# Queries and keys of three of four head groups as seven block products instead of eight

## The chip, the cores and the metric

The kernel runs on one core of one Trainium2 chip, as one program that computes the whole block for eight batches. The metric is the device time of one execution in microseconds (us). A core has five engines that run side by side and meet through semaphores: TensorE (PE, matmuls into the eight PSUM banks), VectorE (DVE), ScalarE (ACT), GpSimd (POOL), and SyncE (SP), which here issues the DMAs. [...]

## The reference

An attention block and a feed-forward block, both with a layer norm before and after and a residual sum, in float32. Batches B=8, positions S=1024, model width D=512, 16 heads of 32, feed-forward width 2048.

```python
qvk = (layernorm(x) @ Wqvk).reshape(b, s, 3, H, HD)
q, v, k = qvk[:, :, 0], qvk[:, :, 1], qvk[:, :, 2]
scores = (einsum('bshi,bthi->bsth', q, k) + causal_mask) / sqrt(d)
weights = softmax(scores, axis=2)
x = x + layernorm(einsum('bsth,bthi->bshi', weights, v).reshape(b, s, d) @ Wo)
hidden = layernorm(x) @ W1 + b1
act = relu(hidden + coef * sin(theta + hidden * 0.1))      # coef from the parameters
x = x + layernorm(act @ W2 + b2)
```

The change is about `q` and `k`, the first line of this.

## The kernel before, in words

The sixteen heads are worked on in four groups of four (`g` = 0 to 3), so that the 128 columns of a group's queries fill the 128 partitions, head by head in rows of 32. For each batch `attention` walks through the four groups; the feed-forward of the batch follows, and within it the end of the attention of this batch and the preparation of the next are interleaved.

**Order.** PE, DVE, ACT and POOL run their instructions in the order in which the program text issues them (`in_order`). Work is written as Python generators; `advance(work, n)` issues the next `n` steps of one between other instructions. So what stands next to what is written by hand. While group g is in attention, the generator `project_qkv(b, g + 1)` (or the first group of the next batch) is drawn step by step as filler between the score units.

**One group.** `find_maxima` first computes scores query by key (matmuls at L575) in seven units of four PSUM banks each, in four runs (`MAX_RUNS`): the first run is one unit, the other three are two units each. DVE takes the row maxima out of the banks (L593 and L605), and ACT exponentials of the first half give row sums (L625). After run n, `advance(work, MAX_FILL[g > 0][n])` draws filler. Then the maxima are split into three bf16 parts (on POOL for the first half of the queries) and transposed on PE (L115). Two further units of scores (`MAX_LATE`) come a little later, `later(0)` and `later(1)`.

Then `weigh` computes the scores transposed, key by query, with the maxima folded in by a bf16 matmul (L681, then L692), in ten units (`KEY_UNITS`, counted by `at`): three for the first half of the queries, seven for the second. ACT exponentiates them out of PSUM (L707), POOL sets what lies above the diagonal to zero (`affine_select`, L711), and one unit later PE multiplies them with the values (L730, `flush`). In the second half DVE also adds up the weights (L759), which PE sums over partitions at the start of the next group (L745).

**The projection before.** Queries and keys of a group are each two halves of 512 positions. Each is four matmuls of 128x128 by 512 (the four row blocks of the 512 input features), accumulated in one bank (L477) and copied to SBUF by ACT with the scale (L488). Each takes two steps of filler, two matmuls a step. Values are four steps (L497, L505), two blocks of 128 positions each. A matmul in float32 shows as two records in the trace.

**PSUM.** `psum` hands out banks at build time, in the order of the program: the one that was released longest ago. A unit of scores takes four of the eight banks.

**Other users of the same engines.** In batch 0 `mix_weights` prepares the feed-forward weights with 32 POOL operations of 128x512 (L284) and stores them, one step per weigh unit. The feed-forward works with seven products for eight already, for both of its matrices (`w1_mixed`, `w2_mixed`), its sums made on DVE and POOL (L1125 for the activations).

Of the kernel before, what the change touches and what calls it, by code (L numbers as in the profile page):

```python
# [11 lines left out]
F32 = mybir.dt.float32  # L12
# [20 lines left out]
def kernel(  # L33
# [24 lines left out]
    NG = NH // HPG  # L58
    QSCALE = 1.0 / math.sqrt(D)

# [6 lines left out]
    tp = ctx.enter_context(tc.tile_pool(name="tp", bufs=4))  # L67
    pp = ctx.enter_context(tc.tile_pool(name="pp", bufs=19))
    tmp = ctx.enter_context(tc.tile_pool(name="tmp", bufs=5))
    small = ctx.enter_context(tc.tile_pool(name="small", bufs=4))  # L70
    wp = ctx.enter_context(tc.tile_pool(name="wp", bufs=WEIGHTS))
    mixp = ctx.enter_context(tc.tile_pool(name="mixp", bufs=2))
    sump = ctx.enter_context(tc.tile_pool(name="sump", bufs=4))
# [37 lines left out]
    def in_order(instruction):  # L111
        tc.keep_in_program_order(instruction)
# [20 lines left out]
    w1_mixed = dram.tile([NSTEP, len(PRODUCTS), P, 2 * 2 * P], F32, tag="w1m", name="w1_mixed")  # L133
    w2_mixed = dram.tile([NSTEP, len(PRODUCTS2), P, 2 * QUART], F32, tag="w2m", name="w2_mixed")
    wqvk_v = w_qvk.rearrange("(kc p) n -> p kc n", p=P)

# [5 lines left out]
    def fetch(b, g, queue=nc.sync):  # L142

        for part in (0, 1, 2):
            w_of[b, g, part] = w_tile([KC, P], "wqvk")
            c0 = part * D + g * P
            queue.dma_start(w_of[b, g, part], wqvk_v[:, :, c0 : c0 + P])

    fetch(0, 0, nc.scalar)
# [215 lines left out]
    def advance(work, steps=1):  # L365
        for _ in range(steps):
            if next(work, None) is None:
                return

    def finish(work):  # L370
        for _ in work:
            pass
# [22 lines left out]
    def norm1_first():  # L395

        dst = new_xnT(0)
        return staged(NT, *norm_stages(lambda t: xt[0, t], dst, nc.scalar.copy))

    moments_ahead = {}  # L400

# [59 lines left out]
    def project_qkv(b, g):  # L461
# [11 lines left out]
        def queries_or_keys(n, half):  # L473
            pq = psum([P, HALF])
            for kc in range(KC):
                in_order(
                    nc.tensor.matmul(  # L477
                        pq,
                        w_of[b, g, 2 * n][:, kc, :],
                        xnT[b, half][:, kc, :],  # L480
                        start=(kc == 0),
                        stop=(kc == KC - 1),
                    )
                )
                if kc == 1:
                    yield True
            dst = qk[b, g][n][:, half * HALF : (half + 1) * HALF]
            in_order(nc.scalar.activation(dst, pq, AF.Copy, scale=1.0 if n else -QSCALE))  # L488
            drained(pq)
            yield True  # L490

        def values(t0):
# [12 lines left out]
            in_order(nc.scalar.copy(v[b, g][:, t0 : t0 + 2, :], pv))  # L505
            drained(pv)
            yield True

        yield from queries_or_keys(0, 0)
        yield from values(0)  # L510
        yield from queries_or_keys(1, 0)
        yield from queries_or_keys(0, 1)
        yield from queries_or_keys(1, 1)
        for t0 in (2, 4, 6):
            yield from values(t0)

# [8 lines left out]

    MAX_FILL = ((3, 2, 2, 2), (1, 2, 2, 2))

# [239 lines left out]
    def attention(b, wvT, after):  # L770
# [24 lines left out]
        for g in range(NG):  # L795
            more, first = after(g)
            mT, later = find_maxima(b, g, work, sums, more if first is None else iter(()))
            mTs = [mT]
            at = 0
            for c in range(2):  # L800
# [3 lines left out]
                for u, keys in enumerate(units):  # L804
                    later(at)
                    weights, placed = weigh(b, g, c, keys, mTs[c])
                    if at < 2:
                        advance(work)
# [6 lines left out]
                    if c and u == len(units) - 2:  # L815
                        finish(work)
                        work = projections(g + 1)
                    if c and u >= len(units) - 2:
                        advance(work)
# [51 lines left out]
    def finish_block(b, half, wvT, x2T, mixed, out_w):  # L871


        x2T[half] = tp.tile([P, KC, HALF], F32, tag="t", name=f"x2T_{b}_{half}")
        mixed[half] = mixp.tile([P, 3, 2, QUART], F32, tag="mix", name=f"mix_{b}_{half}")
        ys, xns, mvs, rss = {}, {}, {}, {}
# [48 lines left out]
        def mix(t):  # L925
# [5 lines left out]
            b12, b22 = right[:, :2], right[:, 2:]  # L931
            m1, m2, m4 = (mixed[half][:, n, :, t * P : (t + 1) * P] for n in range(3))
            subtract = lambda *a: in_order(nc.gpsimd.tensor_tensor(*a, ALU.subtract))
# [8 lines left out]
    def feed_forward(b, x2T, mixed, before, between):  # L942
# [49 lines left out]
        def product(bank, s, name, first=False):  # L992
# [6 lines left out]
                "3": x[:, 2:, QUART:],  # L999
                "4": m[:, 2],  # L1000
                "5": m[:, 0],
                "6": m[:, 1],
                "7": x[:, :2, QUART:],
# [247 lines left out]
        advance(between)  # L1251
        finish(before)
        units = second()
        advance(units)
        for s, quota in enumerate(SECOND):
# [3 lines left out]
            for n, more in enumerate(quota):  # L1259
# [9 lines left out]
                if s == STEPS and n == 3 and b + 1 < B:  # L1269
                    fetch(b + 1, 1)  # L1270
        finish(measuring)
        while len(quarters) > 1:
            advance_ends(1)
# [4 lines left out]
    advance(first_norm, TPB + 4)  # L1278
    for _ in range(TPB):
        advance(work)  # L1280
        advance(first_norm)
    finish(first_norm)
    advance(work, 4)
    prepare_parameters()
# [71 lines left out]
```

## Time and profile before

| | |
|---|---|
| median of 3 runs | 3681.44 us (3680.97 to 3681.45) |
| the profiled execution | 3681.3 us |
| its span, first to last instruction | 3679.6 us |
| PE busy | 3601.1 us, 98% |
| DVE busy | 2680.4 us, 73% |
| ACT busy | 1408.2 us, 38% |
| POOL busy | 1133.8 us, 31% |
| mean granted clock of PE | 0.997 |

A row of a group gives the line, the engine, the operation, output and input tiles with their shapes and the number of records; then the busy time of all and the mean of one in ns; then the engine's idle time before them and what ended it. A row of the timeline gives start and duration in us, the engine, line and operation, and the number of records merged; in brackets the idle time before it and what ended that. A row of the windows gives the stretch, its length, then the busy time of PE, PE's weight loads, DVE, ACT and POOL, then the granted clock of PE (1.00 is full), the DMA share and GB/s. Ends of matmuls are modelled, and a matmul that waits for a bank can show as a long matmul.

### The profile page before, as it was taken

To read this page: it belongs to the slowest core of one execution; us is meant where nothing else is said; L and a number is where in the kernel's file an instruction comes from. 1 tells how busy PE (TensorE), PEld (TensorE's weight loads), DVE (VectorE), ACT (ScalarE), POOL (GpSimd) and SP (SyncE) were. 2 spreads that over 40 slices of the span, in tenths; PEclk is the share of its full clock that TensorE was granted. 3 is DMA by queue.
4 is the path that set the end of the run, shared out by engine and by line. 5 is a ranking of instruction groups with operands and counts; after the bars stand their busy time and mean duration, and the time that the engine had idled before them with its cause. 6 is when DMAs were issued, how large, how long until landed. Compare 5 with 4: busy or idle time off the path is not lost.

```text
span 3679.6 us, 61558 instructions
## 1 busy us (share of the span) xinstructions
PE 3601.1 (98%) x22721; PEld 2357.4 (64%) x22721; DVE 2680.4 (73%) x5571; ACT 1408.2 (38%) x2708; POOL 1133.8 (31%) x1740
## 2 busy tenths in 40 slices
PE   8999999999999999999999999999999999999998
PEld 4447864478654786548854488544885458854587
DVE  5877867678676786767867678776787767777775
ACT  4552135621355213652146521465114642156410
POOL 2333432134311343113431234222342223422243
PEclk9999999999999999999999999999999999999999
DMA  4444751047510574105841068310683116820176
GB/s 137 142 141 132 243 192 34 20 146 249 175 41 10 158 258 154 41 10 172 266 132 41 13 185 269 112 41 18 198 275 92 38 33 199 262 70 13 47 220 197
DMA packets 305084, 476.21 MB, mean 129 GB/s; under 512 B 29136, under 2 KB 90640, under 8 KB 304784
## 3 DMA queue, kind: packets, MB, share of 16 engines
q1 hardware_dynamic: 302624, 470.44, 40.8%
q8 instruction: 181, 2.97, 0.3%
q10 hardware_dynamic: 2160, 1.84, 0.2%
q14 instruction: 119, 0.97, 0.1%
HBM read 440.70 MB, written 31.46 MB: 128 GB/s over the span
## 4 chain that ended last, share of the span: by engine, by line
PE 83%; DVE 11%; ACT 2%; POOL 2%; issue 1%; DMA 0%; POOLq 0%; DVEq 0%; SPq 0%; ACTq 0%
PE banks L1144 16%; PE banks L1009 15%; PE banks L477 13%; PE banks L575 8%; PE banks L730 7%; PE banks L692 7%; PE banks L497 7%; PE banks L897 6%; PE banks L681 3%; PE banks L115 2%; DVE u L1036 2%; DVE hid L1052 2%; DVE u L1030 1%; PE banks L745 1%; DVE hid L1058 1%; ACT w L707 1%
## 5 line engine op out<-in xcount | busy, mean ns | idle before, releaser
L707 ACT ACTIVATE w<-banks 128x1024 f32<-128x1024 f32 (+1 forms) x640 | 566.6, 939 | 296.1 <-PE banks L692 296.0
L759 DVE TENSOR_TENSOR w<-w 128x1024 f32<-128x1024 f32 (+3 forms) x400 | 421.9, 1099 | 186.7 <-PE banks L730 151.8
L711 POOL TENSOR_SCALAR_AFFINE_SELECT w<-w 128x256 f32<-128x256 f32 x512 | 287.3, 578 | 847.2 <-ACT w L707 839.8
L605 DVE CUSTOM_DVE_ANT_0 es<-banks,mask 128x128 f32<-128x128 f32 (+3 forms) x1024 | 432.5, 485 | 102.6 <-PE banks L575 102.6
L1009 PE MATMUL banks<-x2T,wm 128*128 128x256 f32 x2048 | 477.3, 381 | 28.1 <-DVE u L1079 13.6
L477 PE MATMUL banks<-xnT,wqvk 128*128 128x512 f32 x1024 | 481.3, 609 | 0.7 <-ACT xnT L342 0.7
L1144 PE MATMUL banks<-wm,hm 128*128 128x256 f32 x2048 | 470.4, 380 | 2.3 <-POOL hm L1125 2.3
L1037 ACT ACTIVATE u<-u 128x1024 f32<-128x1024 f32 x128 | 135.3, 1057 | 852.1 <-DVE u L1036 803.5
L1009 PEld LDWEIGHTS banks<-x2T,wm 128*128 128x128 f32 x2048 | 386.7, 190 | 91.0 <-DVE u L1079 16.8
L1144 PEld LDWEIGHTS banks<-wm,hm 128*128 128x128 f32 x2048 | 388.0, 190 | 56.4 <-POOL hm L1125 5.5
L593 DVE TENSOR_REDUCE mx<-banks 128x1 f32<-128x512 f32 (+1 forms) x384 | 309.8, 862 | 109.1 <-PE banks L575 109.1
L1144 PE MATMUL banks<-wm,hid 128*128 128x256 f32 x1536 | 357.7, 379 | 0.0
L1009 PE MATMUL banks<-mix,wm 128*128 128x256 f32 x1536 | 354.6, 380 | 2.3 <-DVE u L1079 2.3
L1125 POOL TENSOR_TENSOR hm<-hid 128x256 f32<-128x256 f32 x256 | 204.0, 797 | 456.2 <-DVE hid L1058 437.9
L477 PEld LDWEIGHTS banks<-xnT,wqvk 128*128 128x128 f32 x1024 | 182.8, 190 | 239.1 <-issue 184.5
L692 PE MATMUL banks<-q,k 32*128 32x512 f32 (+3 forms) x3072 | 329.6, 491 | 0.0
L730 PE MATMUL banks<-w,v 128*32 128x512 f32 (+3 forms) x3072 | 318.5, 495 | 5.4 <-POOL w L711 5.4
L1009 PEld LDWEIGHTS banks<-mix,wm 128*128 128x128 f32 x1536 | 291.1, 190 | 50.6 <-issue 7.6
L575 PE MATMUL banks<-k,q 32*128 32x512 f32 (+3 forms) x3072 | 322.0, 513 | 0.4 <-DVE mx L605 0.2
L1144 PEld LDWEIGHTS banks<-wm,hid 128*128 128x128 f32 x1536 | 292.4, 190 | 39.1
L625 ACT ACTIVATE es<-es,mx 128x512 f32<-128x512 f32 (+3 forms) x512 | 279.6, 550 | 2.1 <-DVE mx L605 2.1
L497 PEld LDWEIGHTS banks<-wqvk,xnT 128*128 128x128 f32 x2048 | 239.3, 192 | 51.6 <-issue 24.4
(114 smaller groups left out, 4322.9 us busy)
## 6 DMA issues: line engine op xcount, KB each, us to landing
wm<-w_mixed SPq DMA_DIRECT2D x1344, 256.0 KB, 3.1
xin<-in_L_attn_h_dram SPq DMA_DIRECT2D x112, 256.0 KB, 3.8
wqvk<-in_L_attn_Wqvk_dram SPq DMA_DIRECT2D x93, 256.0 KB, 5.2
out_dram<-x SPq DMA_DIRECT2D x64, 256.0 KB, 2.1
x<-in_L_attn_h_dram SPq DMA_DIRECT2D x60, 256.0 KB, 3.1
w_mixed<-w_t SPq DMA_DIRECT2D x56, 256.0 KB, 3.0
wo<-in_L_attn_Wo_dram SPq DMA_DIRECT2D x32, 256.0 KB, 5.0
w_t<-in_L_ffn_W_dram SPq DMA_DIRECT2D x32, 128.0 KB, 4.0
```

The lines of the kernel that those rows point to most:

```text
L477: nc.tensor.matmul(pq, w_of[b, g, 2 * n][:, kc, :], xnT[b, half][:, kc, :], start=(kc == 0), stop=(kc == KC - 1),)
L497: nc.tensor.matmul(pv[:, t - t0, :], xnT[b, t // TPB][:, kc, (t % TPB) * P : (t % TPB + 1) * P], w_of[b, g, 1][:, kc, :], start=(kc == 0), ...
L575: nc.tensor.matmul(scs[j // 2][:, j % 2, at : at + n], queries[r, i * P : (i + 1) * P], keys[r, k0 : k0 + n], start=True, stop=True,)
L593: nc.vector.tensor_reduce(out=mx[:, m], in_=sc[:, m, cols], op=ALU.min, axis=mybir.AxisListType.X,)
L605: nc.vector.tensor_tensor_reduce(out=es[:, m, cols], in0=sc[:, m, cols], in1=mask[:, HALF - n :], scale=1.0, scalar=FMAX, op0=ALU.add, op1 ...
L692: nc.tensor.matmul(sts[j // 2][:, j % 2, cols], all_keys[r, kb * P : (kb + 1) * P], all_queries[r, q0 : q0 + n], start=False, stop=True,)
L707: in_order(nc.scalar.activation(w[:, :, :width], st[:, :, :width], AF.Exp, scale=-1.0))
L711: select = nc.gpsimd.affine_select(out=square, in_=square, compare_op=ALU.is_ge, fill=0.0, base=0, pattern=[[0, 2], [1, P]], channel_multi ...
L730: nc.tensor.matmul(acc[r, HALF - n :], v[b, g][:, kb, r], weights[j // 2][:, j % 2, cols], start=first and k == 0, stop=last and k == len( ...
L759: in_order(nc.vector.tensor_add(t[:, :, q], t[:, :, q], w[:, :, cols]))
L1009: nc.tensor.matmul(bank[:, n, :], w[:, n, kc, :], moving[:, kc, :], start=first and kc == 0 and n == 0, stop=kc == 1 and n == 1, skip_grou ...
L1144: nc.tensor.matmul(region, a[:, n], w[:, n], start=start and n == 0, stop=last and n == 1, skip_group_check=True,)
```

## The change

The eight block products of a group's queries and keys (two halves of the input features, two halves of the positions, queries and keys) become seven, by the scheme of Strassen and Winograd, for the groups 1, 2 and 3 of each batch. Group 0 is projected as before, though in whole steps.

- Four sums of blocks of the normalised input (`mix_x`, eight POOL operations of 128x512) are made once a batch: for batch 0 before the first group, for the others in the last two steps of the feed-forward of the batch before.
- Four sums of the weights of a group (`mix_weights_of_group`, four POOL operations of 128x256) are made in batch 0, stored to DRAM and fetched again for each later batch, two more loads of 256 KB a group.
- Each of the seven products is two matmuls into a bank of its own. ACT copies it to SBUF with the scale, and POOL makes the sums, seven operations of 128x512 a group. The scale 1/sqrt(D) is split evenly over queries and keys.
- The filler now has eight steps, not twelve: values, two products, values, values, two products, values, two products, one product. `MAX_FILL` and the places in `attention` where filler is drawn are changed to suit.
- The pool `pp` has 24 buffers, not 19; the feed-forward's `mixed` tiles lie in it too, and the pool `mixp` is gone.

```diff
-    QSCALE = 1.0 / math.sqrt(D)
+    HALF_SCALE = float(D) ** -0.25
-    pp = ctx.enter_context(tc.tile_pool(name="pp", bufs=19))
+    pp = ctx.enter_context(tc.tile_pool(name="pp", bufs=24))
-    mixp = ctx.enter_context(tc.tile_pool(name="mixp", bufs=2))
+    qk_mixed = dram.tile([NG, 2, P, 4 * P], F32, tag="qkm", name="qk_mixed")
...
+        if b and g:
+            for n in range(2):
+                w_of[b, g, "mix", n] = w_tile([4 * P], "wmix")
+                queue.dma_start(w_of[b, g, "mix", n], qk_mixed[g, n])
...
+    def mix_weights_of_group(b, g):
...
+        pool(s12[:, near], wk[:, near], wk[:, far], ALU.add)
+        pool(s12[:, far], s12[:, near], wq[:, near], ALU.subtract)
+        pool(s34[:, near], wq[:, near], wk[:, near], ALU.subtract)
+        pool(s34[:, far], wq[:, far], s12[:, far], ALU.subtract)
+        for n in range(2):
+            nc.sync.dma_start(qk_mixed[g, n], w_of[b, g, "mix", n])
+    def mix_x(b):
...
+        for to, left, right in ((t1, b12, b11), (t2, b22, t1), (t3, b22, b12), (t4, b21, t2)):
+            for kc in range(2):
+                in_order(
+                    nc.gpsimd.tensor_tensor(to[:, kc], left[:, kc], right[:, kc], ALU.subtract)
+                )
+                yield True
...
+        def product(w, kc0, moving, dst, sign=1.0):
+            pq = psum([P, HALF])
+            for kc in range(2):
+                in_order(nc.tensor.matmul(pq, w[:, kc0 + kc, :], moving[:, kc, :],
+                                          start=kc == 0, stop=kc == 1))
+            in_order(nc.scalar.activation(dst, pq, AF.Copy, scale=sign * HALF_SCALE))
+            drained(pq)
+        def blocks():
...
+            product(wq, 0, xnT[b, 0][:, :2, :], p1)
+            product(s12, 2, t2, p6)
+            add(p6, p6, p1)
+            u2 = p6
+            yield True
+            values(2)
+            yield True
+            values(4)
+            yield True
+            p2, p7 = pair()
+            product(wq, 2, xnT[b, 0][:, 2:, :], p2, -1.0)
+            product(s34, 0, t3, p7)
+            subtract(queries[:, near], p2, p1)
+            add(p7, p7, u2)
+            u3 = p7
+            yield True
+            values(6)
+            yield True
+            p5, p4 = pair()
+            product(s12, 0, t1, p5)
+            product(wk, 2, t4, p4)
+            add(keys[:, near], p4, u3)
+            add(keys[:, far], p5, u3)
+            add(p5, p5, u2)
+            u4 = p5
+            yield True
+            p3, _ = pair()
+            product(s34, 2, xnT[b, 1][:, 2:, :], p3, -1.0)
+            subtract(queries[:, far], p3, u4)
+            yield True
+        values(0)
+        yield True
+        if g:
+            yield from blocks()
+        else:
...
-    MAX_FILL = ((3, 2, 2, 2), (1, 2, 2, 2))
+    MAX_FILL = ((2, 1, 1, 1), (1, 1, 1, 1))
...
+            if not b and g + 2 < NG:
+                mix_weights_of_group(b, g + 2)
...
-                    if at < 2:
+                    if at in (1, 4):
                         advance(work)
...
-                    if c and u >= len(units) - 2:
+                    if c and u == len(units) - 1:
                         advance(work)
...
+        mixing_x = mix_x(b + 1) if b + 1 < B else iter(())
...
+                if s >= STEPS - 1:
+                    advance(mixing_x)
```

## The prediction

> **What bounds the kernel now.** I read the page first, then the timeline of TensorE and VectorE in one attention group, then the same stretch where the kernel happens to have no filler.
>
> ```profile
> PE 3601.1 (98%) x22721; PEld 2357.4 (64%) x22721; DVE 2680.4 (73%) x5571; ACT 1408.2 (38%) x2708; POOL 1133.8 (31%) x1740
> L477 PE MATMUL banks<-xnT,wqvk 128*128 128x512 f32 x1024 | 481.3, 609 | 0.7 <-ACT xnT L342 0.7
> ```
>
> TensorE (PE) is busy 98% of the span; the query and key products (L477) are 481.3 us of it. The profiled run took 3681.3 us, its span 3679.6; the median of the runs is 3681.44, so sums made on the span carry over as they stand. Does PE set the time in each stretch? The windows of two equal stretches (first score unit to the first late pair of units: maxima and their filler) say no:
>
> ```profile
> core 0: us, PE busy (x) PEld busy (x) DVE busy (x) ACT busy (x) POOL busy (x), PEclk, DMA share, GB/s
> 1468.82:1497.97 29.15, 29.15 (x219) 16.00 (x217) 22.77 (x77) 15.46 (x44) 2.26 (x8) 1.00 0.07 19
> 3390.19:3414.67 24.48, 23.96 (x147) 13.00 (x145) 23.81 (x79) 13.01 (x38) 2.25 (x8) 0.79 0.00 1
> ```
>
> The second is the last group of the last batch, with nothing left to project. Without the 16.7 us of projections that the first one holds, it is only 4.7 us shorter: VectorE (DVE), busy 23.81 of 24.48, is the bound there. PE still reads 98% busy, so its busy share does not show waiting. The kernel is PE-bound only because each filler is as long as DVE needs:
>
> ```profile
> 1472.87 2.00 PE L575 MATMUL banks<-k,q 32*128 32x512 f32 x16
> 1474.80 3.70 PE L477 MATMUL banks<-xnT,wqvk 128*128 128x512 f32 x8
> 1478.43 2.00 PE L575 MATMUL banks<-k,q 32*128 32x512 f32 x24
> 1474.03 2.42 DVE L593 TENSOR_REDUCE mx<-banks 128x1 f32<-128x512 f32 x3 [0.60 <-PE banks L575]
> 1479.59 2.42 DVE L593 TENSOR_REDUCE mx<-banks 128x1 f32<-128x512 f32 x3 [0.70 <-PE banks L575]
> ```
>
> Scores and filler take PE 5.56 us (1472.87 to 1478.43); DVE, 1.16 us behind, needs 4.84 for that run's maxima (1474.03 to 1478.87) and 5.17 for the next (1479.59 to 1484.76). It idles 0.4 to 0.7 a run. There is no more slack than that.
>
> **Saved.** 481.3/1024 is 0.470 us a record, two records per matmul; a product over two 128-row blocks is four records, 1.88 us. Seven for eight in 24 groups (three of four, eight batches): -45.1 us.
>
> **The maxima.** The new fills after runs 0 to 3 are two products, values, values, two products: 3.63, 1.98, 1.98, 3.53 us, where 1.98 and three times 3.6 stood. With run 0 at time 0, run 1 now starts at 1.08+0.99+3.63=5.70 (before 4.05); DVE starts at 6.86 and has freed run 2's last bank at 6.86+4.84+5.17=16.87. PE wants that bank for the second half of run 3 at 5.70+1.93+1.98+1.94+1.98+0.97=14.50. Eight banks, four to a unit, leave no other. The wait is 2.4 us, of which I give 0.3 back because the other heads' matmuls overlap it: 2.05 us x 24 = 49.2. The group that projects for the next batch keeps a key filler of 3.63 between: 0.8 x 7 = 5.6.
>
> **The late pair.**
>
> ```profile
> 1491.63 1.14 PE L575 MATMUL banks<-k,q 32*128 32x512 f32 x8
> 1492.59 0.40 PE L681 MATMUL banks<-mT,minus 32*128 32x512 bf16 x4
> 1492.81 1.04 PE L692 MATMUL banks<-q,k 32*128 32x512 f32 x8
> 1493.78 2.05 PE L497 MATMUL banks<-wqvk,xnT 128*128 128x128 f32 x16
> 1495.76 1.14 PE L575 MATMUL banks<-k,q 32*128 32x512 f32 x8
> ```
>
> The order of the changed program has no values product (L497) between the two late units, and both use the same four banks. DVE frees the fourth 1.16+2.45=3.6 us after the first unit starts; PE is back after 2.15 (1491.63 to 1493.78). Wait 1.5, less 0.5 of overlap: 1.0 us x 24 groups; 0.1 in the seven where next-batch transposes stand between. 24.7.
>
> **The sums on Pool.** Seven 128x512 operations a group. Four stand where Pool is idle. Three (both halves of the keys, then u4) are queued behind the copy of p4 and ahead of the two selects of the third unit of weights; PE's weighted values wait for those. The row for such an operation:
>
> ```profile
> L284 POOL TENSOR_TENSOR w_t<-w_t x32: 1257/1274/2277, 73.8 to 253.7; 128x512 f32<-128x512 f32 x32
> ```
>
> PE gets there 0.99+0.66+0.32+1.00+1.19=4.2 us after p4; Pool after 0.77 (copy) + 3x1.26 + 0.85 (two selects) = 5.4: 1.2 us x 17 groups, 0.25 x 7 under transposes: 22.2. I take 1.26, since DVE idles there now (5.12 us before 1507.66); at 2.28 it is 3.1 more a group, +52, kept for the upper end. [...]
>
> **The tail.** The last two units had two half products (1.91 each) as cover for exponentials and selects; now one values product. The last batch shows this place with no cover:
>
> ```profile
> 3383.76 1.81 PE L730 MATMUL banks<-w,v 128*32 128x512 f32 x8
> ...
> 3387.48 1.06 PE L730 MATMUL banks<-w,v 128*32 128x384 f32 x12 [0.48 <-POOL w L711]
> 3389.09 1.17 PE L730 MATMUL banks<-w,v 128*32 128x256 f32 x8 [0.56 <-POOL w L711]
> 3390.19 1.15 PE L575 MATMUL banks<-k,q 32*128 32x128 f32 x16
> ```
>
> 3383.76 to 3390.19 is 6.43 us, against 6.91 (1515.74 to 1522.65) with 3.82 of filler in it. Removing all of it gains 0.5, so removing 1.84 gains no more: charge 1.84-0.5=1.3 x 16, 0.2 x 7 beside transposes: 22.2. The 0.23 us wait for ScalarE after the third unit goes where PE comes later anyway: -5.5.
>
> **At nothing.** Three more copies a group (3x0.60=1.8 us) on ScalarE, 32.55 of 53.83 us busy; if it were late, 1.8x24=43. Mixing the next batch's input, eight Pool operations (10.1 us) in the last feed-forward steps: by the program's order those sums are issued dozens of matmuls (77 x 0.466=36 us in one case) ahead of use; uncovered, 7x10.1=71. Two more loads a group and six stores on SP's queue, a group (54 us) ahead against 5.2 us to land; their 42 loads would cost at most that each, 218. Four weight sums of 0.73 before the first selects of batch 0, where Pool waits 6.2. Pool in batch 0 already carries the feed-forward's weights and makes groups 1.9 to 4.4 us longer (58.18 against 53.83 in the second group): +6, between 0 and a repeat of 13.
>
> **Sum.** -45.1+54.8+24.7+22.2+22.2-5.5+6=+79, so 3760 us. Half the waits would leave +17, 3698.
>
> **Rivals.** *PE-bound throughout:* the waits fall into the pipelining of matmuls, and the saving arrives: 3681-45=3636. For it: in the second group PE's waits now sum to 0.23 of 53.83 us. Against: the unfilled stretch. It decides when the waits of a group sum to under 1.88 us; I have about 5. *The clock falls as well:* batch 0 shows a Pool wait of 1.96 us and what follows:
>
> ```profile
> 95.00:99.50 4.50, 2.54 (x36) 1.30 (x36) 4.10 (x5) 0.52 (x1) 4.50 (x5) 1.00 0.60 190
> 99.50:103.00 3.50, 3.50 (x19) 0.97 (x12) 3.50 (x16) 0.47 (x1) 0.45 (x1) 0.51 0.73 203
> ```
>
> The granted clock is 0.51 after it; scores and sums took 3.51 us (98.90 to 102.41) where 2.07 is usual (1468.82 to 1470.89). Once in each of 24 groups: +35, 3795; with Pool at 2.28 as well, 3847. My waits come in pieces of 0.3 to 1.2 us and the 1.5 us one at 156 left the clock alone, so this is not the likeliest. [...] *It does not do what it says:* the built order does have 14 matmuls for 16 in those groups, so no chance is left for this.
>
> **Chances.** Forecast 0.6, clock or contention on top 0.2, PE-bound throughout 0.12, something between with half the waits or fewer 0.08. Range 3695 (half the waits) to 3825 (clock and part of the contention). A difference of 0.2%, 7.4 us, is about what can be told from no change: faster 0.12, same 0.03, slower 0.85.
>
> **What would show it.** The group from one first score unit to the next, 53.83 us in the second group of a batch, should read about 57.3 (-1.9, +2.05, +1.0, +1.2, +1.3, -0.2). DVE should run without a gap from run 1 to run 3, PE show waits on maxima before run 3 and the second late unit, and on Pool's select at the third unit. From the fourth group's first scores to the next batch's, 285.0 us now, should be some 288.6 (1.8 of filler that the group before no longer takes, 0.8, 1.0), with nothing from the feed-forward in it. A group of 52 us would prove the rival right; a clock under 0.98 over the span, the other.

## The result, and the profile after

The changed kernel takes 3837.32 us (median of four runs, 3837.12 to 3838.48), 1.042 times the time before (95% interval 1.041 to 1.044). That is 155.9 us slower; the forecast was 79 us slower, and the time lies above its range. The profiled execution spans 3835.7 us. The page and the groups of TensorE rows (busy time of all in us, mean of one in ns, then idle time and its releaser):

```profile
PE 3703.1 (97%) x22625; PEld 2411.8 (63%) x22625; DVE 2732.2 (71%) x5571; ACT 1450.6 (38%) x2780; POOL 1467.1 (38%) x1984
...
L672 PE MATMUL banks<-k,q 32*128 32x512 f32 (+3 forms) x3072 | 430.5, 522 | 0.7 <-DVE mx L702 0.6
...
L827 PE MATMUL banks<-w,v 128*32 128x512 f32 (+3 forms) x3072 | 352.2, 498 | 41.6 <-POOL w L808 41.3
```

The rows of before that answer to the last two, the scores and the weighted values:

```profile
L575 PE MATMUL banks<-k,q 32*128 32x512 f32 (+3 forms) x3072 | 322.0, 513 | 0.4 <-DVE mx L605 0.2
...
L730 PE MATMUL banks<-w,v 128*32 128x512 f32 (+3 forms) x3072 | 318.5, 495 | 5.4 <-POOL w L711 5.4
```

PE holds 96 records fewer and is busy 102 us more. The same 3072 records of scores went from 322.0 to 430.5 us with hardly any idle time in front (0.4 and 0.7): that is the wait for banks that DVE has not yet read, and it shows as long matmuls, not as idle time (the waits are read one by one below, and the run named *late* takes one of them away). The wait of the weighted values for Pool's selects does show, 5.4 to 41.3.

Where the 156.2 us between the two spans lie, from the first score unit of each group:

| | before | after | difference |
|---|---|---|---|
| start to first scores | 39.4 | 36.8 | -2.6 |
| batch 0 | 464.2 | 495.9 | +31.7 |
| batches 1 to 6, each | 453.8 | 472.4 | +18.6 (112.5 in all) |
| of these: groups 1, 2, 3 | 57.6, 53.8, 57.4 | 61.1, 58.4, 59.4 | +3.5, +4.6, +1.9 |
| fourth group to the feed-forward | 73.7 | 79.3 | +5.6 |
| feed-forward to the next batch | 211.2 | 214.3 | +3.0 |
| batch 7 | 454.3 | 468.9 | +14.6 |

In batch 6 the difference is 19.3, as the end of its feed-forward was 1.2 us shorter before and only 0.6 now, so the six add up to 112.5. The first row is no gain of the change: the same beginning read 37.5 to 39.1 us in *late*, *adds*, *tail* and *nomixx* below. In the second group of batch 3 (first scores at 1538.71) the waits can be read one by one. Timeline, TensorE and VectorE, maxima:

```profile
1546.34 2.05 PE L530 MATMUL banks<-wqvk,xnT 128*128 128x128 f32 x16
1548.32 3.30 PE L672 MATMUL banks<-k,q 32*128 32x512 f32 x24
1551.56 2.05 PE L530 MATMUL banks<-wqvk,xnT 128*128 128x128 f32 x16
1553.54 3.18 PE L672 MATMUL banks<-k,q 32*128 32x512 f32 x24
1556.64 1.98 PE L545 MATMUL banks<-xnT,wqvk 128*128 128x512 f32 x4
...
1555.43 2.42 DVE L690 TENSOR_REDUCE mx<-banks 128x1 f32<-128x512 f32 x3
```

The same two runs before (the first starts at 1478.43, a row that the prediction shows):

```profile
1480.37 3.70 PE L477 MATMUL banks<-xnT,wqvk 128*128 128x512 f32 x8
1484.00 2.01 PE L575 MATMUL banks<-k,q 32*128 32x512 f32 x24
1485.94 3.70 PE L477 MATMUL banks<-xnT,wqvk 128*128 128x512 f32 x8
```

Runs 2 and 3, twenty-four records of scores each, took 1.94 us before and now take 3.24 and 3.10, counted to the start of the next fill: 1.30 and 1.17 of waiting, together 2.47 us. DVE's reduction at 1555.43 has no idle time in brackets, where the rows shown of before had 0.60 and 0.70: DVE is the bound here. The late pair of units, same view:

```profile
1562.34 1.14 PE L672 MATMUL banks<-k,q 32*128 32x512 f32 x8
...
1563.52 1.04 PE L789 MATMUL banks<-q,k 32*128 32x512 f32 x8
1564.38 2.40 PE L672 MATMUL banks<-k,q 32*128 32x512 f32 x7
...
1568.27 1.98 PE L545 MATMUL banks<-xm,wmix 128*128 128x512 f32 x4
```

Where the next fill stood before (the second unit starts at 1495.76, in the prediction's rows):

```profile
1497.97 2.05 PE L497 MATMUL banks<-wqvk,xnT 128*128 128x128 f32 x16
```

From the second unit of scores to the next fill 3.89 us, where 2.21 stood (1495.76 to 1497.97): 1.68 us. Pool's sums and the third unit of weights:

```profile
1572.76 2.50 POOL L565 TENSOR_TENSOR k<-blocks 128x512 f32<-128x512 f32 x2 [1.84 <-ACT blocks L553]
1575.33 1.26 POOL L565 TENSOR_TENSOR blocks<-blocks 128x512 f32<-128x512 f32 x1
1576.55 0.77 POOL L808 TENSOR_SCALAR_AFFINE_SELECT w<-w 128x256 f32<-128x256 f32 x2
...
1577.01 0.99 PE L827 MATMUL banks<-w,v 128*32 128x256 f32 x8 [0.87 <-POOL w L808]
```

Three sums run back to back in front of the two selects, and PE waits 0.87 us for these. Before, the only wait of PE near there was one of 0.23 us for ScalarE:

```profile
1505.31 0.39 PE L681 MATMUL banks<-mT,minus 32*128 32x512 bf16 x2 [0.23 <-ACT w L707]
```

The tail, after and (last two rows) before:

```profile
1590.34 1.35 PE L827 MATMUL banks<-w,v 128*32 128x512 f32 x8
...
1596.04 1.17 PE L827 MATMUL banks<-w,v 128*32 128x256 f32 x8 [0.56 <-POOL w L808]
1597.13 1.15 PE L672 MATMUL banks<-k,q 32*128 32x128 f32 x16
...
1515.74 1.99 PE L477 MATMUL banks<-xnT,wqvk 128*128 128x512 f32 x4
...
1522.65 1.15 PE L575 MATMUL banks<-k,q 32*128 32x128 f32 x16
```

6.79 us for a stretch that took 6.91 before: 1.84 us of filler is gone and 0.12 came back, so 1.72 is lost. With the 1.88 saved, the second group's account is -1.88 + 2.47 + 1.68 + (0.87 - 0.23) + 1.72 = +4.63, against +4.59 measured.

### The profile page after: what moved, and what is told of

It is laid out like the page before. It is cut to its first block, busy times and chain, and to the rows that moved or that the text cites. A ratio compares the mean times of both kernels' runs of the same rounds, so it can differ in the third digit from the quotient of the medians.

```text
span 3835.7 us, 61886 instructions
## 1 busy us (share of the span) xinstructions
PE 3703.1 (97%) x22625; PEld 2411.8 (63%) x22625; DVE 2732.2 (71%) x5571; ACT 1450.6 (38%) x2780; POOL 1467.1 (38%) x1984
## 3 DMA queue, kind: packets, MB, share of 16 engines
q10 hardware_dynamic: 2160, 1.84, 0.2%
## 4 chain that ended last, share of the span: by engine, by line
PE 77%; DVE 10%; POOL 7%; ACT 4%; issue 2%; DMA 0%; SPq 0%; POOLq 0%; DVEq 0%; ACTq 0%
PE banks L1248 17%; PE banks L1113 15%; PE banks L672 9%; PE banks L545 8%; PE banks L827 5%; PE banks L789 5%; PE banks L1001 5%; PE banks L530 5%; PE banks L513 3%; POOL w L808 3%; PE banks L778 2%; PE banks L114 2%; DVE hid L1156 1%; ACT w L804 1%; DVE u L1140 1%
## 5 line engine op out<-in xcount | busy, mean ns | idle before, releaser
L856 DVE TENSOR_TENSOR w<-w 128x1024 f32<-128x1024 f32 (+3 forms) x400 | 449.9, 1174 | 260.2 <-PE banks L827 235.7
L808 POOL TENSOR_SCALAR_AFFINE_SELECT w<-w 128x256 f32<-128x256 f32 x512 | 311.8, 631 | 615.3 <-ACT w L804 608.1
L1113 PE MATMUL banks<-x2T,wm 128*128 128x256 f32 x2048 | 480.6, 382 | 37.5 <-DVE hid L1183 14.7
L672 PE MATMUL banks<-k,q 32*128 32x512 f32 (+3 forms) x3072 | 430.5, 522 | 0.7 <-DVE mx L702 0.6
L827 PE MATMUL banks<-w,v 128*32 128x512 f32 (+3 forms) x3072 | 352.2, 498 | 41.6 <-POOL w L808 41.3
L789 PE MATMUL banks<-q,k 32*128 32x512 f32 (+3 forms) x3072 | 342.5, 496 | 0.0
L672 PEld LDWEIGHTS banks<-k,q 32*128 32x128 f32 x3072 | 207.5, 186 | 167.0 <-DVE mx L702 101.7
L530 PE MATMUL banks<-wqvk,xnT 128*128 128x128 f32 x2048 | 261.2, 281 | 0.0
L1113 PE MATMUL banks<-mix,wm 128*128 128x256 f32 x1024 | 241.9, 379 | 0.0
L1001 PE MATMUL banks<-wo,wvT 128*128 128x512 f32 x512 | 235.7, 600 | 3.2 <-DVE wvT L864 3.2
```

Source lines behind the costliest of these rows:

```text
L530: nc.tensor.matmul(pv[:, t - t0, :], xnT[b, t // TPB][:, kc, (t % TPB) * P : (t % TPB + 1) * P], w_of[b, g, 1][:, kc, :], start=(kc == 0), ...
L672: nc.tensor.matmul(scs[j // 2][:, j % 2, at : at + n], queries[r, i * P : (i + 1) * P], keys[r, k0 : k0 + n], start=True, stop=True,)
L789: nc.tensor.matmul(sts[j // 2][:, j % 2, cols], all_keys[r, kb * P : (kb + 1) * P], all_queries[r, q0 : q0 + n], start=False, stop=True,)
L808: select = nc.gpsimd.affine_select(out=square, in_=square, compare_op=ALU.is_ge, fill=0.0, base=0, pattern=[[0, 2], [1, P]], channel_multi ...
L827: nc.tensor.matmul(acc[r, HALF - n :], v[b, g][:, kb, r], weights[j // 2][:, j % 2, cols], start=first and k == 0, stop=last and k == len( ...
L856: in_order(nc.vector.tensor_add(t[:, :, q], t[:, :, q], w[:, :, cols]))
```

## The experiments

The theory: the products do save PE work, and the loss comes from fills that no longer fit what DVE and Pool need in each place. The rival: the products themselves cost it, by their banks, ScalarE copies and Pool sums. Times are to be held against 3837.3 (after) and about 3681.4 (before); *fitted2*, *best*, *best2* and *best3* have four to ten times each, the others one time, each beside the kernel before, at 3681.2 to 3682.1 (medians).

**first**: two values blocks between run 0 and run 1, the first two products after run 1.

```diff
         def blocks():
...
+            values(2)
+            yield True
             p1, p6 = pair()
...
-            values(2)
-            yield True
```

> The changed kernel with one thing else: in the filler of groups 1 to 3 a step of values comes before the first two products, so that 1.98 us and not 3.63 us of filler stand between the first and the second run of scores. Theory (VectorE's maxima are one chain that starts with the second run and PE waits for its end): the chain starts 1.65 us earlier, PE's wait in the maxima falls by that, the second group of a batch goes from 58.42 to about 56.8 us and the kernel from 3837 to about 3797 (24 groups x 1.65). Rival (the loss is Pool's and ScalarE's work, wherever the fills stand): 58.4 us and 3837 as they are, within 5.

3831.3 us: a miss for the theory's number. The second group gained 0.8 and the first lost 1.4; most of the 6 us gained lie in batch 0. DVE's wait before run 2 and PE's run 3 in the second group show why:

```profile
1546.77 2.42 DVE L690 TENSOR_REDUCE mx<-banks 128x1 f32<-128x512 f32 x3 [0.70 <-PE banks L672]
...
1549.53 3.61 PE L672 MATMUL banks<-k,q 32*128 32x512 f32 x24
```

The long fill now stands behind run 1 and DVE idles again before run 2; the short fill behind run 2 leaves PE waiting in run 3, which takes 3.54 us to the next fill for 1.94 before. So 1.60 us of the 2.47 are still there: moving a fill moves the wait. Before, a fill of 3.6 us stood behind each of runs 1 to 3.

**late**: a fill between the two late units.

```diff
-        advance(work)
...
-                    if at in (1, 4):
+                    if at in (0, 1, 4):
```

> The changed kernel with one thing else: the filler that was drawn after the transposes of the maxima is drawn between the two late units of scores instead. Theory (the second late unit waits for VectorE to free the banks of the first): about 1.7 us off each of the 24 groups without transposes there, the second group 58.42 to about 56.7, the kernel 3837 to about 3797. Rival (the filler is needed after the transposes just as much, as cover for ScalarE's copy of them): the wait only moves, no more than 8 us off the kernel.

3801.9, 35.4 us less, and the row of scores shows where (same columns as above):

```profile
L672 PE MATMUL banks<-k,q 32*128 32x512 f32 (+3 forms) x3072 | 389.6, 526 | 0.4 <-DVE mx L702 0.2
```

430.5 - 389.6 = 40.9 us, or 1.7 in each of 24 groups, the 1.68 read above. The late pair's wait is shown, and the forecast's 1.0 was too small. Not all of it arrives: the second group gained 1.3 of its 1.7 us, as the fill is missed where it stood, after the transposes.

**adds**: Pool's three sums are issued one step later, with p3, behind the selects.

```diff
+            yield True
+            p3, _ = pair()
+            product(s34, 2, xnT[b, 1][:, 2:, :], p3, -1.0)
             add(keys[:, near], p4, u3)
```

> The changed kernel with one thing else: the three Pool sums after p4 are issued a step later, with that of p3, so that they stand behind the selects of the third unit of weights. Theory (PE waits for these selects behind the sums): about 1.3 us off 17 groups, the second group 58.42 to 57.1, the kernel 3837 to about 3815. Rival (the select is late for ScalarE's exponentials, not for Pool's queue): no change, 3837 within 5. Third: the four sums now run beside the additions of weights on VectorE, and what is gained is lost there, 3830 to 3845.

```profile
L827 PE MATMUL banks<-w,v 128*32 128x512 f32 (+3 forms) x3072 | 341.7, 497 | 23.6 <-POOL w L808 23.5
```

3817.8, 19.5 less; PE's wait for selects fell from 41.3 to 23.5. The order of Pool's queue was a cost, near the forecast's 22.2 in sum. That the totals are so close is in part luck: batch 0 gives 7.7 us of it, and the first two groups of a later batch 1.1 and 0.6.

**tail**: p3 drawn at the last unit but one and no more at the fifth, its sum behind the last selects.

```diff
             product(s34, 2, xnT[b, 1][:, 2:, :], p3, -1.0)
+            yield True
             subtract(queries[:, far], p3, u4)
...
-                    if at in (1, 4):
+                    if at == 1:
...
                     if c and u == len(units) - 2:
+                        advance(work)
+                    if c and u == len(units) - 1:
                         finish(work)
                         work = projections(g + 1)
-                    if c and u == len(units) - 1:
                         advance(work)
```

> The changed kernel with one thing else: the product p3 (in the next batch's projection, the last key half) stands before the last unit but one's weighted values and not at the fifth unit; its Pool sum comes after the last selects. Theory (there PE waits for exponentials and selects, which a filler covers): the 1.9 us that it costs at the fifth unit are free here, the second group 58.42 to about 56.9, the kernel 3837 to about 3810. Rival (the last selects end when Pool has done them, and the end of the group is set by Pool): no change within 5.

3798.0, 39.3 less where 27 was expected: 2.5 and 1.1 us in the first two groups of the later batches, and 10.6 in the first three of batch 0, where Pool is most loaded (busy 140.0 of 281.5 us up to the feed-forward in the changed kernel, 89.4 of 282.3 in batch 1). The place matters, but this run also takes p3's sum off Pool's middle, so it doesn't price the tail alone.

**plain**: fills in the eight places of the changed kernel, but eight products for every group and no sums for queries and keys (sums of the input stay).

```diff
-        if g:
+        if g > NG:
             yield from blocks()
```

> The changed kernel's order of fills alone: all groups are projected in the form of group 0 (eight products accumulated in four banks, no block products, none of their Pool sums); the sums of inputs and weights are still made and stored but not used. Theory (the loss comes from the order and the length of the fills): the second group of a batch stands at 58 to 60 us although nothing of the scheme is in it, the kernel at 3830 to 3860. Rival (the loss comes from the block products, their copies and sums): the second group falls to 54 to 55.5 us, the kernel to 3700 to 3740.

3832.1, within the theory's range: PE has the work of the kernel before, and 151 us are lost without any block product of queries and keys or sum of these (21 of them go to the sums of the input, below). So the rival's numbers fall. But the edit does not keep the changed kernel's order, as the expectation says. In the form of group 0 full products (3.63 us) and values (1.98) take turns, so that in the second group 3.63, 1.98, 3.63 and 1.98 us stand behind runs 0 to 3, where the changed kernel has 3.63, 1.98, 1.98 and 3.53. Of that group's waits, 1.30 us in run 2 and 1.69 in the late pair are the changed kernel's; run 3 has none, and PE waits 0.86 for Pool's split of the maxima instead. It shows that filler in eight places can lose this much by itself; that the totals agree within 5 us proves no more, since the orders differ.

**nosums**: seven products, nothing summed.

```diff
-            add(p6, p6, p1)
...
-            subtract(queries[:, near], p2, p1)
-            add(p7, p7, u2)
```

> The changed kernel without the seven Pool sums of a group: the products are copied straight into queries and keys, so that these are not the right ones; all matmuls and copies stay. Theory (VectorE's chain and the fills): only the wait behind the sums goes, some 1.3 us in 17 groups and a little in batch 0, 3837 to 3800-3815, the second group 57. Rival (Pool as a whole sets the time): the second group under 54, the kernel under 3720.

3798.3, 39 under the changed kernel, and the second group reads 57.3: the theory's outcome. In the changed order the sums on Pool cost 39 us. Batch 0's first three groups alone give 18 of these (60.6, 60.4, 62.1 us for 67.6, 67.5, 66.3). It is also 34 under *plain*, but that is not the worth of the seven products, since the fills of the two differ.

**nomixx**: no sums of the input in the feed-forward.

```diff
-        mixing_x = mix_x(b + 1) if b + 1 < B else iter(())
+        mixing_x = iter(())
+            x_mixed[b + 1] = [
+                xnT[b + 1, 1][:, 2 * n : 2 * n + 2, :] for n in (0, 1, 1, 0)
+            ]
```

> The changed kernel without the eight sums of the next batch's input in the feed-forward: from batch 1 on, products that need them take blocks of the input itself, so that their queries and keys are not the right ones. Theory (these sums delay VectorE's and Pool's work of the feed-forward's end): from the first hidden product to the next batch's first scores 214.3 us falls back to 211.2-211.6, the kernel from 3837 to about 3816. Rival (the feed-forward's loss is the two loads a group and the smaller pool of tiles): 214.3 stays within 0.5.

3815.8, 21.5 less, and the feed-forward is back at 211.25 us (210.05 in batch 6, as before). In the changed kernel's timeline Pool runs two of these sums in front of sums that the feed-forward's PE work needs, and VectorE's operations beside them are longer than the same ones before (last three rows):

```profile
1895.13 2.94 POOL L432 TENSOR_TENSOR xm<-xnT,xnT 128x512 f32<-128x512 f32 x2
1898.04 1.17 POOL L1229 TENSOR_TENSOR hm<-hid 128x256 f32<-128x256 f32 x1
...
1898.54 1.81 DVE L1162 TENSOR_SCALAR hid<-hid,prm 128x512 f32<-128x512 f32 x2
1900.28 0.95 DVE L328 TENSOR_SCALAR yb<-yb,mv,rs 128x512 f32<-128x512 f32 x1
1901.26 1.10 DVE L1338 TENSOR_TENSOR x<-x,yb 128x512 f32<-128x512 f32 x1
...
1816.21 1.34 DVE L1058 TENSOR_SCALAR hid<-hid,prm 128x512 f32<-128x512 f32 x2
1817.47 0.53 DVE L324 TENSOR_SCALAR yb<-yb,mv,rs 128x512 f32<-128x512 f32 x1
1818.04 0.69 DVE L1234 TENSOR_TENSOR x<-x,yb 128x512 f32<-128x512 f32 x1
```

Matched one by one from 150 us after the first hidden product of batch 3 on, VectorE's operations take 3.0 us more than before; in *nomixx* the sum is back within 0.04. PE's waits of that stretch, after and (last row) before:

```profile
1907.72 1.99 PE L1113 MATMUL banks<-x2T,wm 128*128 128x256 f32 x8 [1.86 <-DVE hid L1183]
...
1823.69 2.00 PE L1009 MATMUL banks<-x2T,wm 128*128 128x256 f32 x8 [0.57 <-DVE hid L1079]
```

Of the 3.0 us that the feed-forward loses, PE's waits for VectorE take 1.7 (this one, and 0.42 us at 1903.01 that was not there), those for Pool's own sums 0.6 (0.28 to 0.91). So the theory holds, and the larger part (1.7 us) comes by way of VectorE, whose operations are longer beside Pool's sums (1.81 us for 1.34 in the rows above), and the smaller (0.6) by way of Pool's queue.

**fitted**: the changed products and sums in the twelve fill places of before.

```diff
-    MAX_FILL = ((2, 1, 1, 1), (1, 1, 1, 1))
+    MAX_FILL = ((3, 2, 2, 2), (1, 2, 2, 2))
...
-                    if at in (1, 4):
+                    if at < 2:
...
-                    if c and u == len(units) - 1:
+                    if c and u >= len(units) - 2:
```

In `blocks` each product is a step of its own: p1, p6, values, p2, p7, p5, p4, p3, values, nothing, values, values.

> The block products in the fill order of the kernel before: twelve steps again (p1, p6, values, p2, p7, p5, p4, p3, values, nothing, values, values), drawn where that kernel draws them, with the sums on Pool in the maxima, where Pool is idle, and the last four behind the split of the maxima. Theory (the fills were what was lost): most waits go and the saved 1.88 us a group arrives: the second group 52 to 52.8 us, feed-forward 214.3 as in the changed kernel, the kernel at 3665 to 3695. Rival (seven products with their copies and sums cost more than they save wherever they stand): the second group above 54, the kernel above 3720.

3690.5, 146.8 us under the changed kernel with the same products, copies and sums: the theory holds, and the rival falls. In the second group runs 2 and 3 read 1.93 and 1.94 us, the late pair 2.21, the third unit has no wait for Pool and the tail is 6.92, all as in the kernel before. Since the sums on Pool have other places too, the 146.8 us are the worth of the fills and of Pool's order together. The group's own number was missed: it reads 53.26 us (53.84 before), not 52 to 52.8. Left are 21 us of the feed-forward and two waits in this group, 0.57 us at the sum of the weights (DVE's additions end later) and some 0.6 from the transposes, where the empty step is, to the end of the first late unit.

**fitted2**: the empty step taken out, so that the values come one place earlier.

```diff
             subtract(queries[:, far], p3, u4)
             yield True
-            yield True
             values(4)
```

> The seven products in the fill places of the kernel before, as in the run named fitted, with one change: the values that stood behind the first late unit and after the sum are shifted by one place, so that the fill ahead of the two late units takes values(4), the place at the first weights unit takes values(6), and the place at the second takes nothing. Theory (time is set by whether each fill is as long as DVE and Pool need there): in fitted the second group still waited 0.57 us at the sum and 0.58 us after the first late unit, and stood at 53.26 us; one of the two goes, so 52.6 to 53.0 us, the feed-forward unchanged at 214.3 us from its first hidden product to the next batch, in all 3675 to 3685 us. Rival (what remains in fitted is a cost of the products themselves, their banks, copies and sums): the group stays at 53.2 or more and the kernel at 3690.

3700.6 (ratio to before 1.005, 1.0035 to 1.0065), slower than *fitted*: a miss. The second group reads 54.3. The place now left empty is the one that covered the split of the second half's maxima on DVE:

```profile
1510.27 0.40 PE L114 MATMUL banks<-ident_h,parts_q 128*128 128x128 bf16 x4 [1.22 <-DVE parts_q L665]
```

So each of the two places that were left empty costs PE something, some 0.6 us in *fitted* and 1.22 here; what the seven products save must be missing in some place. The other ten were not tried.

**best**: *fitted2*, products in the order p1, p2, values, p3, p6, p7, p5, p4, and the sums of the input at the start of the first group.

```diff
         work = projections(0)
+        if b:
+            finish(mix_x(b))
...
-        mixing_x = mix_x(b + 1) if b + 1 < B else iter(())
+        mixing_x = iter(())
```

> As fitted2, with two more changes: the products are computed in another order (p1 and p2 first, the first half of the queries summed earlier, p4 alone last) with Pool's sums spread, and the sums of the next batch's input are taken out of the last steps of the feed-forward and put at the start of the first group of the batch itself, ahead of Pool's first work there. Theory: the feed-forward goes from 214.3 back to 211.2 us in each of seven batches (21 us), the second group to 52.4 to 53.0 us, the first group no longer than in fitted (56.4 us) since Pool has nothing to do in the first 20 us of a group; in all 3645 to 3665 us, faster than the kernel before. Rival (Pool's 10 us only change place and now hold up the split of the maxima or the first products): the first group grows by 2 us or more, the feed-forward reads 211.2, and the kernel stays at 3670 to 3690.

3679.9, no difference from before that can be told (0.9985 to 1.0004): a miss. The feed-forward is at 211.25 us as expected and the first group grew by only 0.2 against *fitted2*, but the second reads 54.3, with the wait of *fitted2*.

**best2**: *fitted* with the same move of the input's sums.

> As the run named fitted (seven products, four of the twelve places of filler of the kernel before given the values, seven a product, one nothing), with one change: the sums of the next batch's input leave the feed-forward's last steps and stand at the start of the first group of each batch but the first. Theory: the groups stay as in fitted (second group 53.2 to 53.3 us, first at most 0.3 us longer than 56.35), and the feed-forward goes back from 214.3 to 211.25 us in seven batches, 21 us; so 3668 to 3672 us, 0.2 to 0.4% under the kernel before. Rival (product p6 needs the second of these sums within the first 10 us of the group and PE waits for Pool): the first group grows by 1 us or more and the kernel stays at 3677 or above.

3730.0 (ratio 1.013, 1.011 to 1.015): the rival's outcome, the first group at 65.4 us for 56.35. The second product, p6, needs the second sum of the input. Timeline of TensorE, then windows (stretch, length, busy PE, loads, DVE, ACT, POOL, granted clock, DMA):

```profile
1429.70 1.98 PE L548 MATMUL banks<-xnT,wqvk 128*128 128x512 f32 x4
1438.71 3.78 PE L548 MATMUL banks<-xm,wmix 128*128 128x512 f32 x4 [7.02 <-POOL xm L432]
```

```profile
1431.69:1438.71 7.02, 0.00 (x1) 0.00 (x1) 3.64 (x19) 0.60 (x1) 6.85 (x9) 0.85 0.57 168
1438.71:1442.28 3.57, 3.57 (x4) 1.46 (x5) 0.00 (x0) 0.00 (x0) 3.57 (x3) 0.50 0.00 0
```

PE waits 7.02 us, and then computes at clock 0.50, a product in 3.57 us for 1.9.

**best3**: *best2* with the product order of *best*, so that p6 comes fourth.

```diff
-            p1, p6 = pair()
+            p1, p2 = pair()
...
+            p3, p6 = pair()
+            product(s34, 2, xnT[b, 1][:, 2:, :], p3, -1.0)
+            yield True
+            product(s12, 2, t2, p6)
```

> The order of products of the run named best (p1, p2, values, p3, then p6), so that the first product that needs a sum of the input is the fourth and not the second, with the places of filler of the run named fitted (nothing at the sum of the group's second half, values at the two places after it); the sums of the next batch's input at the start of the first group. Theory (in best2 the second product stood in front of the sums and waited 7.0 us for Pool, nothing else was lost): first group 56.4 to 56.7 us, second group 53.2 to 53.3, feed-forward 211.25, kernel 3666 to 3672 us, 0.3% under the kernel before. Rival (what the moved sums take from Pool comes back in other places of the first group): first group 57.5 us or more, kernel 3677 or more.

3667.6 us, 0.9962 times the time before (0.9948 to 0.9975): 14 us, or 0.4%, under the kernel before, as expected. First group 56.5 us, second 53.2, feed-forward 211.25.

```profile
PE 3577.0 (98%) x22625; PEld 2355.0 (64%) x22625; DVE 2704.6 (74%) x5571; ACT 1449.4 (40%) x2780; POOL 1431.6 (39%) x1984
...
L836 PE MATMUL banks<-w,v 128*32 128x512 f32 (+3 forms) x3072 | 318.9, 496 | 8.0 <-POOL w L817 8.0
```

The weighted values cost about what they did before (318.5 and 5.4). Of the 45 us forecast as the saving, 14 arrive.

## Why the prediction was right in direction and wrong in size

In attention the direction and the mechanism hold: PE waits on DVE and Pool once the fills don't fit, and *fitted* against the changed kernel shows it, since there each of these waits reads as before. The error is in the terms. Of the 77 us missed, three terms make 57: the sums of the input (21), the late pair (24, of which 5 in the fourth group) and the tail (12). The waits of the first three groups of batch 3, read as above:

| us a group | forecast | read in groups 1, 2, 3 |
|---|---|---|
| the maxima, runs 2 and 3 | 2.05, 2.05, 2.05 | 1.86, 2.47, 2.47 |
| the late pair | 1.0, 1.0, 0.1 | 1.69, 1.69, 1.11 |
| Pool's sums, third unit | 1.2, 1.2, 0.25 | 1.38, 0.87, 0 |
| the tail | 1.3, 1.3, 0.2 | 2.38, 1.73, 0.1 |

- *Saved, -45.1.* About right in size: product rows (L545 325.5 us and group 0's L513 117.7) come to 443.2 for 481.3, 38 less.
- *The maxima.* The raw chain gave 2.4 and 2.47 was read: the overlap given back (0.3) wasn't there. In the first group it is less, so only 5 us are missed in all. Half of the wait lies in run 2, where the forecast had all of it in run 3. No run took this wait away alone (*first* moved it, *fitted* took all waits away).
- *The late pair.* The 0.5 taken off for overlap wasn't there, and in the third group the transposes of the next batch's input cover only part of it: 1.11 us are left where the forecast had 0.1. *late* took all of this wait away.
- *Pool's sums in front of the third unit.* Right in sum (*adds*: 19.5 for 22.2), with the luck told there. The choice of 1.26 us an operation was right: median 1.27 in after. The trace of before bears out its reason: of the 32 operations at L284, the ten that lie for over 95% of their time beside additions of weights (L759) take 1.44 to 2.28 us, the other 22 1.26 to 1.29.
- *The tail.* The forecast let the stretch get 0.5 us shorter for the fill that is gone; it got 0.12 shorter in the second group and 0.5 longer in the first.
- *The fourth group, +3.6 to the feed-forward.* +5.6 in seven batches, 14 us more. Read there: 1.8 of filler as forecast, 1.30 in the maxima (run 2 alone; forecast 0.8), 1.69 in the late pair (1.0), and 0.85 on Pool's split of the maxima, which was not forecast.
- *At nothing: the sums of the input.* The step that failed outright. The argument looked at when PE uses these sums, and not at what stands behind them in Pool's queue nor at what VectorE does beside them. The feed-forward's own sums wait behind them (PE's waits for these go from 0.28 to 0.91 us) and VectorE's operations get longer (1.81 us for 1.34), and *nomixx* prices it at 21.5 us. The bound written beside it (71) covered this; the value taken (0) didn't.
- *Batch 0, +6.* It grew by 13 more than the other batches, and *nosums*, without Pool's sums, takes 18.7 off it and 3.0 off another batch. In its second group (timeline of Pool and PE) one of the operations that mix the feed-forward's weights (L288) stands between Pool's sums and the selects:

```profile
141.50 1.28 POOL L565 TENSOR_TENSOR k<-blocks 128x512 f32<-128x512 f32 x1
142.86 1.27 POOL L565 TENSOR_TENSOR blocks<-blocks 128x512 f32<-128x512 f32 x1
144.09 1.27 POOL L288 TENSOR_TENSOR w_t<-w_t 128x512 f32<-128x512 f32 x1
145.31 0.77 POOL L808 TENSOR_SCALAR_AFFINE_SELECT w<-w 128x256 f32<-128x256 f32 x2
...
145.77 1.43 PE L827 MATMUL banks<-w,v 128*32 128x256 f32 x8 [2.04 <-POOL w L808]
```

  So the wait is 2.04 us there for 0.87, and the clock falls after it (0.54 over 3.43 us, last section). The forecast's 13, called a repeat, can't be followed either: batch 0 is 10.3 us longer than another batch before. It took the two loads on Pool one by one and never put them in one queue.
- *The other entries at nothing* hold: no row of PE's waits after names a load or ScalarE's copies of the products, and in batch 0's second group Pool still waits 0.56 us for ScalarE between the sums of weights and the first select.
- *Rivals.* PE-bound throughout fell: *fitted* and *best3* come nearer to it only with other fills. *The clock falls as well* holds for batch 0 (mean 0.97), where the long waits are, and for a few single waits later (last section). What the chances call contention, an operation of 2.28 us on Pool for 1.26, did not come in the new sums of queries and keys (longest 1.59); VectorE's additions beside Pool's got longer, 1.96 to 2.08 us for 1.22 (last section).

The signs named ahead: DVE runs without a gap into run 3, and PE waits where it was said to, and in run 2 besides; the mean granted clock is 0.994, so the clock's sign (under 0.98) is not there; the second group reads 58.4 for 57.3; from the fourth group's first scores to the next batch it is 293.6 for 288.6, with 3.0 of that in the feed-forward, where nothing was to be.

What is not settled: for the first three groups (batch 0 counted like the others, batch 7 as a whole) the sum held 47.8 us (79 less 6 for batch 0 and 7 x 3.6), and 85 came. The readings explain some 33 of these 37 (5 maxima, 19 late pair, 12 tail, less 3 for Pool's sums). For the other 4 I read no term. How much of batch 0's 13 is the clock and how much the longer waits themselves, no run parts.

## What to carry to other kernels

PE's busy share says little where matmuls wait inside (98% at 3681 us, 97% at 3837): compare the busy time of the same rows between kernels, and note for each place of filler which engine needs the time. Work that covers another engine is not saved by removing it: here both places of the twelve that were left empty cost something, and even with the old lengths restored 14 of 45 us arrived. An operation put on a queue that runs in order is priced by what stands behind it (19.5 us in *adds*) and by what another engine does beside it (1.7 of the 3.0 us that a feed-forward loses), and goes where that queue idles and its first reader is far off.

## What the runs showed of the hardware that was not expected

The clock. Windows of the changed kernel after the 2.04 us wait of batch 0 and after the 0.87 us wait of a later batch (columns as above):

```profile
145.77:149.20 3.43, 3.43 (x20) 0.99 (x20) 0.00 (x0) 0.59 (x1) 2.75 (x3) 0.54 0.43 157
...
1577.01:1580.50 3.49, 3.49 (x23) 1.38 (x24) 0.00 (x0) 2.89 (x5) 0.31 (x1) 1.00 0.00 0
```

Half rate for some 3.4 us follows waits of 1.96 (before), 2.04 and 7.02 us (*best2*; 6.8 us of it there), not the usual waits of 0.56 and 0.87. The length of the wait doesn't decide alone: PE's wait of 1.86 us for VectorE at the end of the feed-forward is followed by half rate in batches 0, 2 and 5, and not in batches 1, 3 and 4, nor is one of 2.54 us in batch 6. Batches 0 and 3:

```profile
490.78:494.19 3.41, 3.41 (x10) 2.70 (x9) 3.34 (x4) 0.00 (x0) 2.08 (x2) 0.50 0.88 267
1907.72:1911.10 3.38, 3.38 (x16) 2.99 (x17) 3.31 (x4) 0.00 (x0) 2.71 (x3) 1.00 0.86 287
```

From batch 0's first scores to the first product of its feed-forward the mean granted clock is 0.97 in 281.5 us, 0.99 in 252.9 before. What else decides it, no run here shows.

Pool's adds beside DVE. The 72 sums at L565 into blocks have a median of 1.27 us and a longest of 1.59, so the slow end of 2.28 that the range allowed for did not come; the mixing of weights in batch 0 does reach 2.26 (L288: 1.43 to 2.26 us in the 16 operations beside additions of weights, 1.26 to 1.27 in the other 16). It is VectorE that slows beside the new sums: its additions of weights take 449.9 us in the changed kernel (1.17 us each), 417.5 in *nosums* (1.09) and 421.9 before (1.10). In batches 1 to 7 of the changed kernel the 21 additions of 128x1024 that meet Pool's sum into the queries (L566, 1.26 to 1.27 us) take 1.96 to 2.08 us each, where those that meet no sum of Pool's have a median of 1.22. The operations shown under *nomixx* take 1.81, 0.95 and 1.10 us for 1.34, 0.53 and 0.69. What the longer additions cost the kernel no run shows.
